# Neighbour gathers on one Trainium2 core: SyncE fetches one of 32 neighbours row by row in two of three tiles

## The chip, the core and the metric

The kernel runs on one core of one Trainium2 chip. The core has TensorE (PE, with its weight loads PEld), VectorE (DVE), ScalarE (ACT), GpSimd (POOL) and SyncE (SP), each with an instruction queue of its own, and 16 DMA engines. SyncE computes nothing; it issues DMAs. The metric is the device time of the whole program in microseconds, a median over runs.

## What is computed

Each of 50,001 items has two geographic embeddings of 32 floats, E_in and E_out (packed side by side as one row of 64 floats, 256 B, in `egeo`), and a list of 32 neighbours. For both embeddings an attention of the item over its neighbours is computed:

```
V      = E[near_full]                                  # (n, 32, 32)
w      = softmax(einsum('nd,nkd->nk', E, V) / sqrt(32))
a      = einsum('nk,nkd->nd', w, V)                    # a_sus from E_in, a_inf from E_out
h      = concat(E_hist[history], a_sus[history], a_inf[history])   # (16384, 100, 128)
t      = concat(E_tgt[target], a_inf[target], a_sus[target])       # (16384, 128)
scores = relu((h * t) @ W1.T + b1) @ W2
attn   = exp(scores) * mask / sum(...) ** 0.5
s      = sum(h * attn);   out = sigmoid(cosine(s broadcast, t))
```

## The kernel before

There are two stages. The **item stage** (lines 113 to 359) works out a_sus and a_inf for all items and writes two tables of rows to DRAM (`table` and `ttab`). The **user stage** (lines 362 to 509) gathers 100 rows of `table` for each of 16,384 users and scores them.

The item stage goes over 391 tiles of 128 items, one item to a partition: 23 iterations (`it`) of 17 tiles (`j`), with `s = 17*it + j`. A tile's neighbours go into `v`, 128 x 32 x 64 floats, of which there are five buffers. The 32 neighbours come in two ways:

- Neighbours k = 0 to 29: one indirect DMA from GpSimd for each k, in `gather` at L215. It takes 128 indices from `nidx` and brings one row of 256 B to each partition.
- The last two (`NAUX` = 2): the whole of `egeo` stands transposed in SBUF as `geoT`, two items to a column. ScalarE copies 128 columns for one of the neighbours, VectorE 128 for the other (`columns`, L229), each column at an address in a register. TensorE turns them back (`turn`, L234) and ScalarE and VectorE put them into `v` (`even`, `odd_half`).

The addresses come from `load(it)`, once for 17 tiles: SyncE loads `nidx`, `own` and `row` (L130, L132, L134), VectorE turns the last three neighbour numbers of every item into addresses, TensorE transposes them and they stand in `cols`, one line of 128 numbers for each tile and neighbour. The first of the three lines, byte addresses in `egeo` for neighbour 29, is worked out in the kernel before too, but not used there. `registers` (L189) loads 32 addresses at a time into an engine's registers.

The part of `gather` that the change touches:

```python
k1 = K - NAUX - 1
by_sp = s * SPNUM % SPDEN < SPNUM
if by_sp:
    for i0 in range(0, P, NREG):
        vals = registers(s, 0, E.SP, i0, 0, (ITEMS - 1) * 8 * G)
        for i in range(NREG):
            nc.sync.dma_start(
                v[i0 + i : i0 + i + 1, k1].rearrange("p t d -> p (t d)").bitcast(U8),
                egeo_b[:, ds(vals[i], 8 * G)],
            )
for k in range(k1 if by_sp else k1 + 1):
    nc.gpsimd.indirect_dma_start(...)          # L215
```

The order of the item stage is written out by hand (`manual_schedule`), tile by tile, in a loop over s (L337). In step s the tile s is gathered and its columns copied; `turn`, `even`, `odd_half`, `products` (L258), `scores` and `exponents` work on tile s-1, `weighted` (L294) and `attend` (L309) on tile s-2, and `finish` on tile s-3. A buffer of `v` is free once `weighted` has read it. In the middle of an iteration (s mod 17 = 8) `load` for the next one is issued, ahead of that tile's `gather`. After the last tile of an iteration ScalarE issues the two stores, L325 to `table` and L326 to `ttab`. Ahead of the loop SyncE loads `egeo` in 66 pieces (`st`, L171), out of which TensorE makes `geoT`.

DMAs of SyncE and ScalarE share eight semaphores in turn, those of GpSimd another eight. A DMA that takes a semaphore waits until the one that held it before, eight DMAs earlier, has landed.

Of the kernel before, what the change touches and what calls it, by code (L numbers as in the profile page):

```python
# [36 lines left out]

AUX = ("AAAA", "DDDD",)
NAUX = len(AUX)
SPNUM, SPDEN = 0, 1  # L40
ENGINE = {"A": E.Activation, "D": E.DVE}
NREG = 32
PAIRS = ROWS // 2
# [554 lines left out]
```

## Time and profile before

| | |
|---|---|
| Median of 3 runs | 30856.08 us (30855.88 to 30856.29) |
| Profiled execution | 30865.45 us, span 30863.6 us |
| GpSimd busy in the span | 23284.3 us (75%) |
| Gathers of neighbours, L215 | 11730, mean 944 ns |
| Gathers of history rows, L438 | 12800, mean 944 ns |
| Register loads of 32 addresses, L189 | 1564 on ScalarE, 1564 on VectorE |
| End of the item stage | about 14,690 us |

The page gives busy time for each engine over the whole span. Register loads, semaphore instructions and the issuing of DMAs by SyncE and ScalarE do not count as busy; they are seen in the timeline of the engine and in the view of a line (with a q behind the engine's name). A name such as L215 is a line of the kernel. "Idle before" is the time that an engine did nothing just before a group's instructions, with what ended that wait; "issue" means that the profile shows nothing it waited for.

### The profile page before, as it was taken

The page shows a single profiled execution, that of the slowest core. Times are in us where ns is not written, and L with a number is a line of the kernel's source. Part 1 is how long each engine was busy: PE and PEld are TensorE (multiplying, and loading weights), DVE is VectorE, ACT ScalarE, POOL GpSimd, SP SyncE. Part 2 cuts the span into 40 slices and gives each one's busy share as a digit, 9 for nine tenths or more (in the row PEclk, how much of TensorE's full clock was granted, in tenths as well). Part 3 has the DMA queues.
Part 4 walks back from the last instruction along what each step waited for, and adds up shares of the span by engine and source line. Part 5 has one row for each costly group of instructions (what it writes and reads, how often), then busy time and mean ns, then how long its engine had stood idle before and what let it go on. Part 6 is the DMA issues. An engine that isn't in the chain of part 4 may idle for free.

```text
span 30863.6 us, 246685 instructions
## 1 busy us (share of the span) xinstructions
PE 13340.6 (43%) x45932; PEld 7630.5 (25%) x45932; DVE 12128.8 (39%) x58485; ACT 7843.2 (25%) x56963; POOL 23284.3 (75%) x24664
## 2 busy tenths in 40 slices
PE   0000000000000000000778778877877877887787
PEld 0000000000000000000444444444444544454444
DVE  5555555555555555555222222222222222222222
ACT  4333333333333333333111111111111111111111
POOL 7777777777777777777777777777777777777777
PEclk9999999999999999999665666666566566656656
DMA  2111111111111111111222222222222222222221
GB/s 67 31 31 31 32 34 31 31 31 32 34 31 31 31 35 31 31 31 29 54 53 54 54 53 54 53 53 53 54 53 54 53 54 53 53 53 54 53 54 52
DMA packets 966199, 1351.82 MB, mean 44 GB/s; under 512 B 548416, under 2 KB 561280, under 8 KB 961696
## 3 DMA queue, kind: packets, MB, share of 16 engines
q0 software_dynamic: 789056, 1233.20, 17.1%
q10 hardware_dynamic: 103920, 51.31, 0.6%
q1 hardware_dynamic: 71664, 51.54, 0.6%
q14 instruction: 1192, 9.76, 0.1%
q8 instruction: 367, 6.01, 0.1%
HBM read 1295.95 MB, written 51.30 MB: 44 GB/s over the span
## 4 chain that ended last, share of the span: by engine, by line
POOL 56%; issue 23%; DMA 12%; PE 7%; DVE 1%; another core or an unknown queue 0%; ACT 0%; POOLq 0%; SPq 0%; ACTq 0%; DVEq 0%
POOL v L215 33%; POOL h L438 23%; DMA h<-table,hidx 10%; PE z_ps L473 3%; DMA v<-in_egeo_dram,nidx 2%; PE score L482 2%; PE hT_ps L453 2%; DVE xT L455 1%; DVE hsum L458 0%; DMA st<-in_egeo_dram 0%; PE pt L180 0%; POOL t L400 0%; POOLq L438 0%; ACT g L229 0%
## 5 line engine op out<-in xcount | busy, mean ns | idle before, releaser
L438 POOL DMA_INDIRECT h<-table,hidx x12800 | 12084.6, 944 | 3899.7 <-issue 3451.0
L215 POOL DMA_INDIRECT v<-in_egeo_dram,nidx x11730 | 11078.2, 944 | 3599.4 <-issue 3484.2
L453 PE MATMUL hT_ps<-ident,h 128*128 128x128 f32 x12800 | 5070.5, 414 | 3207.2 <-DMA h<-table,hidx 3025.5
L455 DVE TENSOR_TENSOR xT<-hT_ps,tT 128x1024 f32<-128x1024 f32 (+1 forms) x1664 | 1968.4, 1183 | 10942.7 <-PE hT_ps L453 10942.5
L234 PE MATMUL pt<-ident,g 128*128 128x128 f32 x782 | 363.9, 471 | 13297.0 <-DVE g L229 8118.8
L473 PE MATMUL z_ps<-xT,w1T 128*128 128x512 f32 x6400 | 5799.9, 1007 | 26.6 <-DVE xT L455 26.3
L229 ACT COPY g<-geoT 128x4 uint8 x50048 | 4919.0, 189 | 2153.7 <-issue 2152.4
L474 ACT ACTIVATE z<-z_ps,b_sb 128x512 f32<-128x512 f32 x3200 | 2201.1, 688 | 12756.3 <-PE z_ps L473 12748.7
L229 DVE COPY g<-geoT 128x4 uint8 x50048 | 3885.9, 194 | 2268.1 <-issue 2149.5
L453 PEld LDWEIGHTS hT_ps<-ident,h 128*128 128x128 f32 x12800 | 2439.0, 194 | 8517.2 <-DMA h<-table,hidx 7853.9
L482 PEld LDWEIGHTS score<-w_sb,z 128*128 128x128 f32 x25600 | 4330.9, 255 | 0.6 <-issue 0.5
L482 PE MATMUL score<-w_sb,z 128*128 128x1 f32 x25600 | 4022.1, 279 | 0.1
L234 PEld LDWEIGHTS pt<-ident,g 128*128 128x128 f32 x782 | 141.9, 183 | 13514.9 <-DVE g L229 8226.4
L258 DVE TENSOR_TENSOR prod<-v,own_ps 128x2048 f32<-128x2048 f32 x391 | 894.4, 2287 | 4148.8 <-DMA v<-in_egeo_dram,nidx 4147.6
L458 DVE TENSOR_REDUCE hsum<-h 128x8 f32<-128x1024 f32 (+1 forms) x1664 | 1942.6, 1167 | 0.0
L473 PEld LDWEIGHTS z_ps<-xT,w1T 128*128 128x128 f32 x6400 | 1884.4, 354 | 115.0 <-issue 70.4
L294 DVE TENSOR_TENSOR wv<-v,ex 128x1024 f32<-128x1024 f32 x782 | 1404.3, 1869 | 0.0
L281 ACT ACTIVATE ex<-sc,top 128x32 f32<-128x32 f32 x782 | 227.7, 291 | 4355.4 <-DVE top L273 4342.8
L268 DVE TENSOR_REDUCE sc<-prod 128x64 f32<-128x2048 f32 x391 | 894.5, 2288 | 13.5
L309 DVE TENSOR_REDUCE att<-wv 128x64 f32<-128x2048 f32 x391 | 882.9, 2258 | 0.0
L240 ACT COPY v<-pt 128x128 f32<-128x128 f32 x391 | 104.0, 266 | 2520.2 <-PE pt L234 2520.2
L489 DVE TENSOR_TENSOR ea<-ea,keep 128x100 f32<-128x100 f32 x128 | 33.8, 264 | 1177.1 <-ACT ea L488 1177.1
(67 smaller groups left out, 1536.8 us busy)
## 6 DMA issues: line engine op xcount, KB each, us to landing
h<-table,hidx POOLq DMA_INDIRECT x12800, 2.5
v<-in_egeo_dram,nidx POOLq DMA_INDIRECT x11730, 2.4
table<-row ACTq DMA_DIRECT2D x23, 1088.0 KB, 4.5
own<-in_egeo_dram SPq DMA_DIRECT2D x23, 544.0 KB, 4.0
row<-in_ehist_dram SPq DMA_DIRECT2D x23, 544.0 KB, 6.4
ttab<-trow ACTq DMA_DIRECT2D x23, 544.0 KB, 6.1
ttab<-in_etgt_dram ACTq DMA_DIRECT2D x1, 12500.0 KB, 52.4
st<-in_egeo_dram SPq DMA_DIRECT2D x65, 192.0 KB, 2.4
```

The source lines that it names most:

```text
L215: nc.gpsimd.indirect_dma_start(out=v[:, k].rearrange("p t d -> p (t d)"), out_offset=None, in_=egeo, in_offset=bass.IndirectOffsetOnAxis(a ...
L229: copy(g[:, 4 * i : 4 * i + 4], geoT_b[:, ds(vals[i - i0] - geoT_at, 4)])
L258: nc.vector.tensor_tensor(prod.rearrange("p k t d -> p k (t d)"), v.rearrange("p k t d -> p k (t d)"), subs[s]["own"].to_broadcast([P, K, ...
L268: nc.vector.tensor_reduce(sc.rearrange("p t k -> p k t"), subs[s]["prod"], AX.X, ALU.add)
L294: nc.vector.tensor_tensor(subs[s]["wv"][:, t].rearrange("p d k -> p k d"), subs[s]["v"][:, :, t, :], subs[s]["ex"][0][:, t, :] .rearrange( ...
L438: nc.gpsimd.indirect_dma_start(out=h[:, q, :], out_offset=None, in_=table, in_offset=bass.IndirectOffsetOnAxis(ap=u["hidx"][:, l : l + 1], ...
L453: nc.tensor.transpose(hT_ps[:, q, :], h[:, q, :], ident)
L455: x = nc.vector.tensor_tensor(xT[:, 0:w, :], hT_ps[:, 0:w, :], u["tT"].to_broadcast([D, w, P]), ALU.mult)
L458: s = nc.vector.tensor_reduce(u["hsum"][:, g * LW : g * LW + w], h[:, 0:w, :], AX.X, ALU.add)
L473: nc.tensor.matmul(z_ps, w1T, xT[:, q : q + LG, :], start=True, stop=True)
L474: nc.scalar.activation(z[:, q : q + LG, :], z_ps, AF.Relu, bias=b1_sb)
L482: nc.tensor.matmul(u["score"][:, l : l + 1], z[:, q, :], w2_sb, start=True, stop=True)
```

## The change

Two constants: `by_sp` is now true for two of three tiles, those with s mod 3 = 0 or 2. For them GpSimd gathers neighbours 0 to 28 only. Neighbour 29 is fetched by SyncE: four times 32 addresses into registers, and 128 DMAs of one row of 256 B each, from `egeo` to one partition of `v`.

```diff
 AUX = ("AAAA", "DDDD",)
 NAUX = len(AUX)
-SPNUM, SPDEN = 0, 1
+SPNUM, SPDEN = 2, 3
 ENGINE = {"A": E.Activation, "D": E.DVE}
 NREG = 32
```

GpSimd issues 261 gathers fewer in the item stage (11,469 in place of 11,730); SyncE issues 33,408 DMAs and 1,044 register loads more. On SyncE's queue they stand where `gather(s)` stands in the loop, so the first follow the 66 loads of `st`, and each `load` follows those of the tile before it. Nothing else is changed.

## The prediction

> **What bounds the kernel now.** I read the page first, for the share of each engine and the costliest groups. Columns of a group: line, engine, operation, tiles, count | busy us, mean ns of one | idle us before it and what ended it.
>
> ```profile
> span 30863.6 us, 246685 instructions
> PE 13340.6 (43%) x45932; PEld 7630.5 (25%) x45932; DVE 12128.8 (39%) x58485; ACT 7843.2 (25%) x56963; POOL 23284.3 (75%) x24664
> ...
> L215 POOL DMA_INDIRECT v<-in_egeo_dram,nidx x11730 | 11078.2, 944 | 3599.4 <-issue 3484.2
> ```
>
> POOL is busy 75% in every slice, and what is missing to 100% is called "issue": the gap between one gather and the next. The timeline of POOL inside the item stage shows this as a fixed beat (start us, length us):
>
> ```profile
> 5039.23 0.95 POOL L215 DMA_INDIRECT v<-in_egeo_dram,nidx  x1 [0.30 <-issue]
> 5040.48 0.94 POOL L215 DMA_INDIRECT v<-in_egeo_dram,nidx  x1 [0.30 <-DMA v<-in_egeo_dram,nidx]
> 5041.73 0.94 POOL L215 DMA_INDIRECT v<-in_egeo_dram,nidx  x1 [0.30 <-issue]
> ```
>
> One gather costs POOL 1.2495 us (2401 of them in the 3000 us of the next view), and a tile has 30: 37.49 us. Times 391 tiles this is 14,658 us, and the last item tile ends near 14,690 us. So POOL alone sets the item stage. The groups of a 3000 us window (80 tiles) show how far the others are behind:
>
> ```profile
> L215 POOL DMA_INDIRECT v<-in_egeo_dram,nidx x2401 | 2269.1, 945 | 731.6 <-issue 713.0 <-DMA v<-in_egeo_dram,nidx 18.6
> L229 ACT COPY g<-geoT 128x4 uint8 x10240 | 1006.5, 189 | 442.9 <-issue 442.7
> L229 DVE COPY g<-geoT 128x4 uint8 x10240 | 792.3, 194 | 440.7 <-issue 440.3
> ...
> L258 DVE TENSOR_TENSOR prod<-v,own_ps 128x2048 f32<-128x2048 f32 x80 | 183.0, 2287 | 878.7 <-DMA v<-in_egeo_dram,nidx 878.7
> ```
>
> VectorE waits 878.7/80 = 11.0 us in every tile for the gathers to land. ScalarE waits 918.3/80 = 11.5 us in that window for VectorE's score maximum and more elsewhere. Both could take a tile faster by 1.25 us. The DMA engines are busy to 0.16 of their time between 200 and 14,690 us.
>
> SyncE is not in the table of busy times. Its own timeline and the views of two lines (duration ns min/median/max) give the price of an issue:
>
> ```profile
> 5124.25 0.33 SPq L130 DMA_DIRECT2D nidx<-in_near_dram  x1
> 5124.69 0.38 SPq L132 DMA_DIRECT2D own<-in_egeo_dram  x1
> ...
> L171 SPq DMA_DIRECT2D st<-in_egeo_dram x66: 327/328/1667, 53.8 to 169.1; - x66
> ...
> L189 ACTq TENSOR_LOAD <-cols x1564: 1948/1978/5590, 171.7 to 14631.3; - x196
> ```
>
> Between its three loads for each 17 tiles SyncE only waits (11,865.8 us at L130 for gathers), so the queue is free. The last line is the load of 32 addresses into registers.
>
> **The change part by part.**
>
> *POOL, removed.* Tiles with s*2 mod 3 below 2 are 261 of 391; each loses its 30th gather. 261 x 1.2495 = 326.1 us, all on the path. Three tiles (two fetched by SyncE) go from 90 gathers, 112.46 us, to 88, 109.96 us.
>
> *SP, added.* A fetched tile costs SyncE 4 register loads and 128 one-row copies of 256 B, each a DMA. All are issued in order, and the copies wait for nothing new except the semaphore of the copy eight before (DMAs of SyncE and ScalarE take eight semaphores in turn) and, at the first row of a tile, v's free buffer. The loads: 4 x (1.98 + 0.045 to the next instruction) = 8.1 us; the first row's waits, five semaphore instructions of about 0.06 us as in the loads of before, 0.3 us. So 8.4 us fixed, plus 128 c, with c from the start of one copy to the start of the next. SyncE has 109.96/2 = 54.98 us for each fetched tile if the gain is to come whole: **c must be under 0.364 us**. It breaks even with the old beat at 56.23 us: **c = 0.374 us**. Everything hangs on c, and the trace has no one-row copy at an address from a register.
>
> Bounds of c. Nearest are the static copies of 128 contiguous rows: 0.328 + 0.045 = 0.373 us, the break-even itself. Dearer: own, the dearest of that shape in the steady state, 0.376 + 0.045 = 0.421; the burst at the very start, where 128-row copies follow each other without waiting, starts them at 0.75, 1.19 and 1.66 us, so 0.44 and more. A copy of 17x128 rows (row, L134) takes 0.545. So an issue grows with the shape that it has to walk: +0.217 us for one more level. A copy of one run has a level less than the cheapest row, and may be spared what 128-row copies pay right behind each other (own: 0.332 us at its shortest, 0.376 in the median, behind nidx); against that stands the reading of a register. From below c is held by the ring of eight: a copy lands 2.0 us after its issue at best (the smallest of st, and b_sb), 2.4 us in the median of st, so 2.0/8 = 0.25 and 2.4/8 = 0.30 us. Between 0.25 and 0.42 I take the middle, **c = 0.335**, 10% under the nearest row for the level that is gone. Then a fetched tile costs SyncE 128 x 0.335 + 8.4 = 51.3 us of the 54.98: 93% full, and POOL still sets the pace.
>
> [...]
>
> *SP, moved past.* The loads of the next 17 tiles (nidx, own, row) now stand behind the row copies of the eighth tile. They are issued some eight tiles (about 290 us) before they are read, and the buffers that they waited for are free by then: nothing. If SyncE fell behind for good, they would be late with everything else.
>
> *ACT and DVE.* The stores of table and ttab (L325, L326) take semaphores of the same ring, so ScalarE waits there, once in 17 tiles, until a row of SyncE has landed, with its exponents and column copies queued behind; and SyncE then waits for the store to land (4.5 and 6.1 us). Covered by the 11.5 us of ScalarE and, for SyncE, by 3.7 us spare in each of some 11 fetched tiles. If the cover were gone: at most 23 x 6.1 = 140 us. The product (L258) waits for eight semaphores more, some 0.5 us of VectorE's 11.0 us.
>
> *Transfers.* The same 8.6 MB move, as 33,408 single rows. At a share of 0.16 there is room; a gather waits for its eighth predecessor, 10 us back, and lands in 2.4, so slower landings cost POOL nothing.
>
> *The start.* SyncE reaches the first row only after the 66 loads of st (169.7 us). The first fetched tile lands near 169.7 + 51.3 + 2 = 223 us; before, its product began at 194.0 us and POOL, which had stopped for a buffer, went on at 214.75 us, 20.7 us later. Now that is near 244: +29 us, and the 3.75 us saved in tiles 0, 2 and 3 are lost in that wait. After this SyncE gains on POOL (tiles 7 and 8 are just in time).
>
> **Sum.** -326 + 29 + 4 = -293 us. The profiled execution took 30,865.45 us (span 30,863.6), 9 us over the median of the runs, 30,856; I count from the median: **30,563 us**. The user stage from 14,690 us on is not touched.
>
> **The rivals.**
> - *SyncE becomes the bound.* Decides from c = 0.374. For it: the nearest row is at that point, and the opening burst is above it. Against: those copies name 128 rows. With own's 0.421: 62.3 us, three tiles 124.6, +12.1 x 130.3 = +1,580, so 32,436 us; with the burst's 0.44, 33,070 us. At 17x128 rows' 0.59 it would be 38,000, which I hold unlikely: one row has fewer levels.
> - *The ring of eight.* If single rows land later than 2.9 us (eight times 0.364), landing and not issue paces SyncE. nidx takes 2.8 us, with 17 times the bytes a row: just enough. At 3.2 us c is 0.40 and the run 31,740 us.
> - *A tie.* c between 0.372 and 0.375: 30,856 us. A narrow window.
> - *It gains in part.* c from 0.364 to 0.372: SyncE paces, 30,580 to 30,800 us.
>
> **How the numbers follow.** Gain whole or nearly so 0.50, in part 0.08, tie 0.04, slower by issue 0.30, by the ring 0.08. A measurement of this kernel tells 0.2% (62 us) from no change. So faster 0.58, same 0.04, slower 0.38. The likeliest case's own range is 30,520 to 30,640. The range must take in most of the slower side: low 30,500 (the whole 326 us, a little below), high 33,100 (c = 0.44); above lies about 0.12.
>
> **What would show it.** POOL gathers 11,469 at the old beat of 1.25 us, three tiles in 110 us; POOL's waits at L215 for a v buffer only at the start, some 45 us; SyncE's copies at L210 under 0.32 us long. I am wrong if SyncE shows no idle time in the stage and POOL waits at L215 for VectorE in each round.

## The result, and the profile after

The changed kernel takes 30,566.05 us in the median (30,565.43 to 30,567.29) against 30,856.19 us for the kernel before: a ratio of 0.9906, with a 95% interval of 0.989 to 0.9922. 290 us are gone; 293 had been forecast, and 30,563 us.

The page of the profile after, with the lines that answer to those shown of before:

```profile
span 30564.2 us, 318469 instructions
...
L215 POOL DMA_INDIRECT v<-in_egeo_dram,nidx x11469 | 10824.7, 944 | 3557.6 <-issue 3344.7
...
v<-in_egeo_dram SPq DMA_DIRECT2D x33408, 0.2 KB
```

The 261 gathers are gone and each of the others costs what it did. Busy and idle of this group make 14,382.3 us, against 11,078.2 + 3,599.4 = 14,677.6 before: 295.3 us less. The other large group of POOL, the history gathers of the user stage, before and after:

```profile
L438 POOL DMA_INDIRECT h<-table,hidx x12800 | 12084.6, 944 | 3899.7 <-issue 3451.0
L438 POOL DMA_INDIRECT h<-table,hidx x12800 | 12078.8, 944 | 3900.9 <-issue 3299.3
```

They make 15,984.3 us and 15,979.7 us. So the two groups hold the whole of the 299.4 us between the two spans, and 295.3 of it lies where the change was made. (The spans differ by 9 us more than the medians because the profiled execution of the kernel before was 9 us over its median.)

In a window of 3000 us inside the item stage POOL still sets the beat, and now gets through 82 tiles instead of 80:

```profile
L215 POOL DMA_INDIRECT v<-in_egeo_dram,nidx x2403 | 2267.8, 944 | 732.9 <-issue 701.2 <-DMA v<-in_egeo_dram 18.6 <-DMA v<-in_egeo_dram,nidx 12.8
...
L258 DVE TENSOR_TENSOR prod<-v,own_ps 128x2048 f32<-128x2048 f32 x82 | 187.6, 2288 | 807.0 <-DMA v<-in_egeo_dram 446.7 <-DMA v<-in_egeo_dram,nidx 348.1 <-ACT g L229 9.6
```

The first line has one gather in 3000/2403 = 1.248 us. The second says who VectorE waits for: more than half of its 807 us now end with a row of SyncE (`DMA v<-in_egeo_dram`), the rest with a gather of POOL. SyncE's rows are often the last to land, but VectorE still has 807/82 = 9.8 us idle in a tile. POOL's waits that are put down to a row, between 300 and 14,400 us (us in total, times, longest):

```profile
POOL v L215 <- DMA v<-in_egeo_dram: 87.3, 286, 0.3
```

None is longer than the 0.30 us that stand before every gather, so POOL does not notice. The page's chain of work puts 11% of the span on SyncE's queue all the same. That is not enough to call SyncE the bound: after the start no gather of POOL came later for it.

What SyncE pays is in the views of its two lines (duration ns min/median/max, first and last start us):

```profile
L210 SPq MOVE v<-in_egeo_dram x33408: 29/29/38, 173.8 to 14362.8; - x199
L210 SPq DMA_DIRECT2D v<-in_egeo_dram x33408: 224/225/1052, 173.9 to 14362.9; - x199
L189 SPq TENSOR_LOAD <-cols x1044: 2027/2172/2442, 171.4 to 14350.5; - x174
```

A row is two instructions: a MOVE of 29 ns and a DMA of 225 ns. From the trace's start times the median from one row to the next is 0.320 us, and from the first row of a fetched tile to the first row of the next one, where both follow without a wait, 51.3 us.

At the start of the stage POOL's timeline shows one long wait. The first line is of the kernel before, the other two of the changed one:

```profile
214.75 0.94 POOL L215 DMA_INDIRECT v<-in_egeo_dram,nidx  x1 [18.97 <-DVE wv L294]
192.09 0.94 POOL L215 DMA_INDIRECT v<-in_egeo_dram,nidx  x1 [0.30 <-issue]
244.72 0.94 POOL L215 DMA_INDIRECT v<-in_egeo_dram,nidx  x1 [51.69 <-DMA v<-in_egeo_dram]
```

The wait is 32.7 us longer, and 326.1 - 32.7 = 293.4 us is, within 2 us, what the group of the change lost.

SyncE needs long to make up for its late start. By the start times in the trace its last row for tile 5 comes 95.6 us after POOL's last gather for that tile, and not before tile 53 are the two level. POOL does not stop in this time, because the five buffers of `v` let it run ahead of SyncE. Later SyncE is ahead, by up to 66 us (1.8 tiles) from its first row of a tile to POOL's first gather of the same tile.

SyncE's own waits, after the start:

```profile
SPq L210 <- DMA table<-row: 727.0, 20, 54.0
...
SPq L210 <- DMA row<-in_ehist_dram: 17.1, 22, 1.4
...
SPq L210 <- DMA v<-in_egeo_dram: 0.4, 2, 0.3
```

Waits of a row on a row eight earlier come to 0.4 us: the eight semaphores are no limit at this pace. The first line is SyncE standing still for ScalarE's store, 36 us each time; more of it below.

One wait is new on VectorE. The first instruction of its work on the addresses of the next 17 tiles (`coli`, L142) now waits for the load of `nidx`; the kernel before shows no such wait:

```profile
DVE coli L142 <- DMA nidx<-in_near_dram: 174.5, 8, 35.4
```

### The profile page after: what moved, and what is told of

Its sections match the earlier page's. It is cut to its first block, busy times and chain, and to the rows that moved or that the text cites. A ratio compares the mean times of both kernels' runs of the same rounds, so it can differ in the third digit from the quotient of the medians.

```text
span 30564.2 us, 318469 instructions
## 1 busy us (share of the span) xinstructions
PE 13360.2 (44%) x45932; PEld 7637.3 (25%) x45932; DVE 12144.3 (40%) x58485; ACT 7840.0 (26%) x56963; POOL 23025.0 (75%) x24403
## 4 chain that ended last, share of the span: by engine, by line
POOL 30%; issue 15%; DMA 14%; SPq 11%; PE 5%; DVE 1%; DVEq 0%; POOLq 0%; ACT 0%; ACTq 0%
POOL h L438 24%; DMA h<-table,hidx 13%; SPq L210 9%; POOL v L215 7%; PE z_ps L473 3%; SPq L189 2%; PE hT_ps L453 1%; PE score L482 1%; DMA v<-in_egeo_dram,nidx 1%; DVE xT L455 1%; DMA row<-in_ehist_dram 0%; DVE g L229 0%; DVE hsum L458 0%; DMA v<-in_egeo_dram 0%; DVEq L189 0%
## 5 line engine op out<-in xcount | busy, mean ns | idle before, releaser
L215 POOL DMA_INDIRECT v<-in_egeo_dram,nidx x11469 | 10824.7, 944 | 3557.6 <-issue 3344.7
L229 ACT COPY g<-geoT 128x4 uint8 x50048 | 4918.5, 189 | 2156.0 <-issue 2145.6
L229 DVE COPY g<-geoT 128x4 uint8 x50048 | 3879.3, 196 | 2246.8 <-issue 2128.7
```

Source lines behind the costliest of these rows:

```text
L215: nc.gpsimd.indirect_dma_start(out=v[:, k].rearrange("p t d -> p (t d)"), out_offset=None, in_=egeo, in_offset=bass.IndirectOffsetOnAxis(a ...
L229: copy(g[:, 4 * i : 4 * i + 4], geoT_b[:, ds(vals[i - i0] - geoT_at, 4)])
```

## The experiments

Four kernels were run, in a later session (on a chip numbered 5; which chip gave the first times is not on record). There the kernel before itself took **40,266.27 us** (40,179 to 40,353, 9 runs), not 30,856. It has no trace of that session; the four kernels' traces show what is different. A gather (947 ns) and a column copy on ScalarE (190 ns) are as long as before, but ScalarE and VectorE (56,963 and 58,485 instructions on the page of `pool_alone`, against POOL's 24,403) and SyncE with its rows stand still between their instructions for stretches. VectorE's timeline, with `pool_alone` (described below) as the example; L223 is there what is L229 in the kernel before:

```profile
5002.24 0.28 DVE L223 COPY g<-geoT 128x4 uint8 x1 [1.29 <-issue]
5003.64 0.17 DVE L223 COPY g<-geoT 128x4 uint8 x1 [1.12 <-issue]
5005.04 0.17 DVE L223 COPY g<-geoT 128x4 uint8 x1 [1.23 <-issue]
5006.45 0.17 DVE L223 COPY g<-geoT 128x4 uint8 x1 [1.23 <-issue]
```

One copy starts every 1.40 us, where in the first session 32 run in 2.4 to 2.7 us. ScalarE's steps in `late_start` are 0.70 to 0.79 or 1.38 to 1.40 us from 5029.55 to 5040.19 us, where 11 us earlier 32 copies ran in 3.15 us: the stretches come and go. SyncE's own records are odd there: in `late_start` its MOVEs are recorded with 1 to 1,397 ns and its DMAs with 1 to 1,526 (in the changed kernel of the first session 29 to 38 and 224 to 1,052), at the same medians of 29 and 225. So a single record of SyncE says little there; its totals over the stage do not depend on that.

The expectations in absolute times, which had 30,856 us in mind, could not be met, and the comparisons below are with 40,266 us. The changed kernel itself was not run in the later session. What the later session shows is the change, or parts of it, where SyncE's rows take far longer on average. From the first history gather to the end the four runs take 20,154 to 20,278 us, so nearly all that tells them apart lies in the item stage.

**SyncE's fetch left out (`pool_alone`).** POOL drops its 30th gather in 261 tiles; SyncE issues one copy of 128 fixed rows in place of the 128 single ones.

```diff
-                for i0 in range(0, P, NREG):
-                    vals = registers(...)
-                    for i in range(NREG):
-                        nc.sync.dma_start(v[i0 + i : i0 + i + 1, k1]..., egeo_b[:, ds(vals[i], 8 * G)])
+                nc.sync.dma_start(v[:, k1].rearrange("p t d -> p (t d)"), egeo[0:P, :])
```

> Only POOL's side of the change: in the 261 tiles POOL drops its 30th gather, and in place of the 128 row copies SyncE issues one copy of 128 fixed rows (neighbour 29 is therefore not the real one). Theory: all of the gain is POOL's beat, so 30856 - 326 + 4 = 30,534 us, 32 us under the changed kernel, because SyncE is ready for the first tile in time. Rival (SyncE's row copies cost something all along): more than 60 us under the changed kernel.

Measured: 39,919.00 us, a ratio of 0.9915 (0.9899 to 0.993), so 347 us under the kernel before of its session. The size is near POOL's 326, but that may be chance and is no proof of the theory, since POOL does not set the beat here. Its group in a window of 3000 us (60 tiles, 50 us each):

```profile
L209 POOL DMA_INDIRECT v<-in_egeo_dram,nidx x1762 | 1668.3, 947 | 1332.9 <-DVE wv L288 798.7 <-issue 533.6 <-DMA v<-in_egeo_dram,nidx 0.6
```

POOL waits 799 us in it for VectorE (`wv`, which frees a buffer of v). Why dropping a gather helps all the same is not settled. The wait at the start cannot be read off either: all is late there.

**POOL's saving left out (`sp_alone`).** POOL keeps all 30 gathers and SyncE's rows go into a spare tile.

```diff
             if by_sp:
+                spare = n_s.tile([P, 2 * G], F32, name="spare")
...
-                            v[i0 + i : i0 + i + 1, k1].rearrange("p t d -> p (t d)").bitcast(U8),
+                            spare[i0 + i : i0 + i + 1, :].bitcast(U8),
-            for k in range(k1 if by_sp else k1 + 1):
+            for k in range(k1 + 1):
```

> Only SyncE's side of the change: POOL keeps all 30 gathers and SyncE's row copies go into a spare buffer that nobody reads. Theory (SyncE's copies run beside everything and cost nothing): 30,856 us, within 30, with SyncE's rows 0.320 us apart. Rival (33,408 more DMAs slow POOL's gathers, or the stores of ScalarE that share semaphores with them hold up the stage): POOL's beat over 1.25 us and the run over 30,920 us.

Measured: 46,016.55 us, a ratio of 1.1434 (1.1418 to 1.145), 5,750 us more. In that session SyncE's side is not free, though nothing reads its rows. SyncE's line:

```profile
L211 SPq DMA_DIRECT2D spare<-in_egeo_dram x33408: 2/225/1580, 284.7 to 25760.0; - x199
```

The median copy still takes 225 ns, and the median MOVE 29. But 33,408 rows fill 25,475 us: 0.763 us for each on average, register loads and the stretches of standing still included, where the first session with its waits had 14,189/33,408 = 0.425. SyncE's waits for others in these 25,475 us come to some 215 us. Its last row starts at 25,760.0 us, its first load of the user stage at 25,760.7, while the last store to `table` was issued at 25,540.6. So SyncE sets the length of the item stage here, though its rows are of no use. The other engines meet it in two places (us in total, times, longest):

```profile
DVE coli L142 <- DMA nidx<-in_near_dram: 3672.9, 22, 208.0
...
ACT g L230 <- DMA ttab<-trow: 2349.8, 22, 110.3
```

The first is VectorE, which needs `nidx` for the next 17 tiles and waits because SyncE's load of it stands behind the rows. The second is ScalarE behind its store, which takes a semaphore of the same round of eight. Among the longest waits of `pool_alone` (down to 1,366 us) neither appears. The two waits can overlap, so how the 5,750 us divide between them stays open, and so does why SyncE stands still for stretches. The rival is half right: the stores do hold up ScalarE, but POOL's gathers are no slower (946 ns and 0.3 us).

**The fetch from the fourth tile on (`late_start`).**

```diff
-            by_sp = s * SPNUM % SPDEN < SPNUM
+            by_sp = s * SPNUM % SPDEN < SPNUM and s >= 3
```

> SyncE fetches in two of three tiles, but not in the first three tiles (259 tiles in place of 261). Theory (the 33 us between the full saving of POOL and the measured one are lost at the start, where POOL waits for SyncE's first rows): POOL waits about 19 us near 195 us as before the change, not 52, and the run takes 30856 - 259 x 1.2495 = 30,532 us. Rival (they are lost through the stage, in ScalarE's stores and in waits for buffers that recur): the run stays at about 30,566 us.

Measured: 45,389.24 us, a ratio of 1.1272 (1.1256 to 1.1287). The question about the start gets no answer here. But the run is, except for two tiles, the change itself in that session, and it **loses** 12.7%. POOL's waits (us in total, times, longest) say why:

```profile
POOL v L215 <- DMA v<-in_egeo_dram: 5848.3, 119, 53.2
POOL v L215 <- DVE wv L294: 4809.0, 263, 131.5
```

and VectorE's product in a window of 3000 us (47 tiles):

```profile
L258 DVE TENSOR_TENSOR prod<-v,own_ps 128x2048 f32<-128x2048 f32 x47 | 107.5, 2288 | 1090.2 <-DMA v<-in_egeo_dram 922.6 <-DMA v<-in_egeo_dram,nidx 127.4 <-issue 38.0
```

Both wait for SyncE's rows. SyncE issues 33,152 rows between 283.8 and 25,137.2 us, 0.750 us each on average, 96.0 us for a fetched tile, and in that time waits for others some 355 us in all. From its first row to the first history gather the run takes 25,163 - 284 = 24,879 us. So SyncE's rows last as long as the stage, and SyncE sets the beat. This is what the first rival of the prediction describes, with an average far beyond its point of 0.374 us. But the cause is not the rival's, a row that is dearer each time: the medians are 29 ns for a MOVE and 225 for a DMA here too. With the register loads (1,036 at a median of 2.15 us) and the waits left out, the mean row is an estimated (24,853 - 2,227 - 355)/33,152 = 0.67 us, twice the 0.320 of the first session, so the time lies in the rows and gaps that are far longer than the median.

**Three tiles of four (`three_of_four`).**

```diff
-SPNUM, SPDEN = 2, 3
+SPNUM, SPDEN = 3, 4
```

> SyncE fetches in three of four tiles (293 or 294 tiles). A fetched tile costs SyncE 128 x 0.320 + 4 x 2.26 + 0.3 = 50.3 us by the trace of the changed kernel; four tiles then need 151 us of SyncE and 146.2 us (117 gathers) of POOL. Theory (the slower of the two queues sets the beat): SyncE is the bound from about its first row at 170 us on, the item stage ends near 170 + 293 x 50.3 = 14,910 us or somewhat later, and the run takes 31,080 to 31,200 us, slower than before the change. Rival (SyncE has more room than that sum): POOL still sets the beat and the run takes 30,856 - 366 + 33 = 30,523 us.

Measured: 47,032.21 us, a ratio of 1.1681 (1.166 to 1.1702). POOL's waits again:

```profile
POOL v L215 <- DMA v<-in_egeo_dram: 8626.4, 178, 160.6
...
POOL v L215 <- DVE wv L294: 3749.8, 206, 64.6
```

With 34 fetched tiles more than `late_start` the waits for SyncE's rows grow from 5,848 to 8,626 us and those for VectorE shrink. The item stage grows by 26,792 - 25,163 = 1,629 us, 48 us for each of the 34. It is less than SyncE's 96 us a tile, because a row is a little cheaper here (26,485/37,504 = 0.706 us). The direction is the theory's (the slower of the two queues sets the beat). Its numbers, 50.3 us of SyncE against 48.7 of POOL, were not tested, for SyncE was the bound in that session with two of three already.

## Why the prediction was right

- **POOL, removed: 326.1 us.** Right. 11,469 gathers at the old 944 ns, and the beat unchanged.
- **SP, added: c = 0.335 us, 51.3 us for a fetched tile.** Measured 0.320 and 51.3. The step held, its parts less so. The DMA alone takes 225 ns, 103 less than the static copies of 128 rows (328), where the prediction took off a tenth; whether this is the level that is gone, no run tells. The register costs an instruction of its own, the MOVE, which with its gap adds some 0.06 us and which the sum did not have. And a load of 32 registers takes 2.17 us on SyncE, not ScalarE's 1.98; with the gaps around the loads the fixed part of a tile is 51.3 - 128 x 0.320 = 10.3 us, not 8.4. The errors cancel, and that the sum came out to the tenth is luck. The c itself was the middle of a range that took in the break-even.
- **The start: +29 us, and 3.75 us lost.** Right to the microsecond: 244.72 us for the end of the wait, where near 244 was said, and 32.72 us more of waiting. This is read from the traces of before and after alone; the run that was to take it away did not decide it. That SyncE then gains on POOL without stopping it again is right too; to draw level takes it until tile 53.
- **SP, moved past: nothing.** Nothing on the path, but misread. The prediction has the loads for the next 17 tiles issued some eight tiles before they are read. VectorE reads `nidx` in the same step in which the load stands, for the addresses. When SyncE is not ahead VectorE waits, eight times and 174.5 us in all. VectorE's slack covered it; in `sp_alone` the same wait is 3,672.9 us.
- **ACT's stores: 4.5 and 6.1 us, covered.** Covered, but mis-sized: SyncE stands still 36 us for a store, not six, and does so 20 times. A store is issued by ScalarE only when it comes to `finish`; SyncE, up to 1.8 tiles ahead, gets to the semaphore long before that and waits for the issue, not only the landing. It loses its lead and wins it back. That cost nothing here, since POOL's waits for rows after the start are 0.3 us each.
- **The ring of eight.** Not a limit, as taken: 0.4 us in all.
- **VectorE's slack.** 11.0 us in a tile before, 9.8 after; right.

The mechanism is therefore the forecast one: POOL lost its gathers at an unchanged beat, and all but the start of it reached the total. That the size came so near rests in part on luck, in c. The prediction gave 0.38 to the slower side, where SyncE is the bound. In the later session, where its rows took more than twice as long on average, it was, and nearly the same kernel lost 12.7%.

Open: what holds the engines up between instructions in that session (whether instructions arrive late, or their recording takes time, no run tells), why `pool_alone` gains, and whether a start at the fourth tile gives the 33 us back where the kernel before takes 30,856 us. The four kernels were not tried there.

## What to carry to other kernels

When one queue sets the beat, work it off to an idle queue by a sum for that queue: its price for one instruction, its fixed cost, and the time that the bound leaves it; the point at which the two cross says what must be known. Here it was 0.364 us by the prediction's fixed cost and (54.98 - 10.3)/128 = 0.349 by the measured one; the change stands at 0.320, with a margin of some 7% for a fetched tile. Ask also what stands behind the new work on the idle queue: here it was the loads of `nidx`, which another engine waits for. A thin margin in the number of issued instructions is a bet on how fast they are issued: the change gains 0.9% in the one session, and nearly the same kernel lost 12.7% in the other, where three engines stood still for stretches.

## What the runs showed of the hardware that was not expected

A copy of one row at an address from a register was cheaper to issue than a static copy of 128 rows: 225 ns and a MOVE of 29, against 328. And the kernel before took 30% longer in another session (40,266 us against 30,856). In the four kernels run there the gathers (947 ns against 944) and ScalarE's column copies (190 against 189) are about as long as in the first session. But ScalarE and VectorE start a column copy only every 0.70 or 1.40 us for stretches, and in the three with rows of SyncE a row takes 0.706 to 0.763 us on average at a median copy of 225 ns, while POOL's gathers still follow each other in 1.25 us where they wait for no buffer.
